# Two more chains for the first image's key offsets, and a later GELU in the first MLP unit

## The chip, the cores and the metric

The kernel runs on one core of a Trainium2 chip. The metric is the device time of the whole kernel in microseconds, in one launch; data is float32 throughout.

## The reference

An image batch x of shape (2, 512, 32, 32) goes through two layers. The first is a deformable attention block with an MLP, the second a plain self-attention. What the change touches lies in the first:

```python
q = _gconv1x1(_bn(x), qw)                                  # 8 groups of 64 channels
off = conv(q as 16 images of 64 channels, off_dw_w, stride 4, pad 1, depthwise)   # 6x6 taps, 8x8 out
off = gelu(off + off_dw_b); off = tanh(einsum('bchw,oc->bohw', off, off_pw_w)) * 4
kv = _grid_sample(xn, grid + off)                          # 64 sampled keys for each group
k, v = _gconv1x1(kv, kw), _gconv1x1(kv, vw)
pos = grid_q[:, :, None] - grid_kv[:, None]                # 1024 queries x 64 keys x 2
bias = sign(pos) * log1p(abs(pos))
bias = relu(relu(bias @ cpb_w1) @ cpb_w2) @ cpb_w3         # 2 -> 128 -> 128 -> 1
attn = softmax(q k^T / 8 + bias); x = x + out_w (attn v) + out_b
h1 = gelu(mlp_w1 _bn(x) + mlp_b1); x = x + mlp_w2 h1 + mlp_b2     # 512 -> 2048 -> 512
```

The second layer is softmax attention over the 1024 positions with four 512 x 512 projections and a residual sum.

## The kernel before, in words

Channels stand on the 128 partitions, so each image has four chunks (b, k) of 128 channels, two groups of 64 in each.

**The main loop.** The bias network takes most of the time. It runs over 256 slots s (one pass of the last loop in the attention part): 16 groups of 16 slots, four keys to a slot, and both images, so that a chunk is needed for 32 slots: chunk (0, 0) in slots 0 to 31, (0, 1) from 32, (0, 2) from 64, (0, 3) from 96, (1, 0) from 128 and so on. In a slot VectorE makes the first hidden layer h two slots ahead (`st_layer1`, L674, into three buffers); TensorE multiplies it by the 128 x 128 weights into four tiles ps of two PSUM banks (L691), of which three buffers exist; ScalarE evicts the four tiles (L701 and L703, into rx, ub and others); VectorE joins them in pairs (`st_sum`, L711); accumulating DMAs on the POOL queue and copies on the SP queue add them over partitions; 22 or 27 slots later TensorE contracts them to the scores (L821). Every fourth slot ScalarE makes tables ta and tb for the next (L654, L662).

**The background.** Beside this a Python generator `bg` does what the later groups need. In each slot whose number allows it, one step is taken, and what it issues is placed behind the second pair of evictions. It runs `chain(ci)` and then `sample(ci)` for each entry of the list CHAINS, in order. A chain has one chunk (K = 1) or two (K = 2). It normalises and projects q, forms the 36 tap products of the depthwise convolution on ScalarE, 12 at a time (`prod`, L381), sums them on VectorE (L396, L401), applies GELU on ScalarE (L405, with a table load), forms the offsets on TensorE (L420, L421) and tanh, log and positions. `TAPS[ci]` says how many taps go into one step; each `yield` ends a step. The result goes to DRAM (`fdr`), from where `load_tables` takes it in the slot with s % 4 = 0 ahead of its use: for chunk (0, 2) in slot 60, for (0, 3) in 92, for (1, 0) in 124. `sample` gathers the keys and makes k and v. The softmax steps of finished groups (`tails`) take every second slot until 60 and then those with s % 4 > 0. Every engine works its own instructions in the order of the program; ScalarE and VectorE serve the loop, the background and the softmax steps out of one queue each.

**The MLP.** Eight units (two images, four parts of the 2048 hidden channels) follow. `layer1` computes a unit's hidden part by a seven-product scheme; six of its products are split again by the same scheme in three sets (`twice`). `twice` orders all steps by a number: set g's products stand at 7 g + 0, 1, 3, 4, 6, 9, 12 (products 1, 2, 6, 5, 7, 4, 3), and other work is put in by its own number. Products 1, 6, 7 and 4 of a set accumulate in one PSUM bank, and each is copied out by ScalarE (L166, L170, L172, L176) before the next may add to it. The hidden blocks go through GELU on ScalarE (L1092). In unit 0, called with `early`, the seventh product is made ahead of all others and parked in r3; `merge` adds it to c11 and applies the GELU to block 0.

The functions that the change touches, and the places that call them:

Of the kernel before, what the change touches and what calls it, by code (L numbers as in the profile page):

```python
# [22 lines left out]
KS = 6  # L23
NG = 16

CHAINS = [[(0, 0)], [(0, 1)], [(0, 2), (0, 3)], [(1, 0), (1, 1)], [(1, 2), (1, 3)]]
TAPS = [36, 6, 4, 3, 3]
NU = 4
INV_BN = 1.0 / (1.0 + 1e-5) ** 0.5
FMAX = 3.4028234663852886e38  # L30
# [27 lines left out]
def conv_seq_kernel(ctx: ExitStack, tc: tile.TileContext, x, xt, kst, pst, cst, vec, wsm, outw, w1, w2, wl, wlt, brow, out):  # L58
# [30 lines left out]
    dp = ctx.enter_context(tc.tile_pool(name="dp", bufs=1, space=bass.MemoryType.DRAM))  # L89
    fdr = [dp.tile([2 * len(g), 4, 2 * W, KT], F32, name=f"fdr{i}") for i, g in enumerate(CHAINS)]  # L90
    chain_of = {c: (i, g.index(c)) for i, g in enumerate(CHAINS) for c in g}
    gdr = [dp.tile([P, NCH, C], F32, name=f"gdr{i}") for i in range(2)]
# [43 lines left out]
    def plus(out, a, b_, op=ALU.add):  # L136
        nc.vector.tensor_tensor(out, a, b_, op)  # L137
# [69 lines left out]
    with tc.tile_pool(name="lp", bufs=2) as lp:  # L207
# [111 lines left out]
        def chain(ci):  # L319
            G = CHAINS[ci]  # L320
            K = len(G)
            (b, k0), n = G[0], 128 * K
            for i in range(K):
                k = k0 + i
# [37 lines left out]
            if ci == 0:  # L362


                taps = sorted(range(KS * KS), key=lambda t: any(a in (0, KS - 1) for a in divmod(t, KS)))
                for m, t in enumerate(taps):
                    for src, dst in pieces(t, acc[:, m % 3]):
                        if m < 3:
                            nc.vector.tensor_scalar(dst, src, col("dww", t), None, ALU.mult)
                        else:  # L370
                            nc.vector.scalar_tensor_tensor(dst, src, col("dww", t), dst, ALU.mult, ALU.add)
            else:


                prod = ph.tile([P, 12, 2, 8, 8], F32, tag="xnt", name="prod")
                nc.gpsimd.memset(prod, 0.0)
                for m in range(3):
                    pr = prod[:, :, 0:K] if K == 2 else prod[:, :, m % 2 : m % 2 + 1]
                    for t in range(12):
                        for src, dst in pieces(12 * m + t, pr[:, t]):  # L380
                            nc.scalar.activation(dst, src, AF.Copy, scale=col("dww", 12 * m + t))  # L381
                        if t % TAPS[ci] == TAPS[ci] - 1:
                            yield
                    rows = ((0, 8, 0, 12),)
                    if m != 1:
                        rows = ((1, 8, 0, 12), (0, 1, 6, 12)) if m == 0 else ((0, 7, 0, 12), (7, 8, 0, 6))
                    for y0, y1, t0, t1 in rows:
                        for k in range(K) if y1 - y0 < 8 else (slice(0, K),):
                            src, dst = pr[:, t0:t1, k, y0:y1, :], acc[:, m, k, y0:y1, :]
                            if y1 - y0 < 8:  # L390
                                src, dst = (src.rearrange("p t y x -> p (y x) t"),
                                            dst.rearrange("p y x -> p (y x)"))
                            else:
                                src, dst = (src.rearrange("p t k y x -> p (k y x) t"),
                                            dst.rearrange("p k y x -> p (k y x)"))
                            nc.vector.tensor_reduce(dst, src, AX.X, ALU.add)  # L396
                    if m < 2 and K == 2:
                        yield
            af = acc.rearrange("p a k y x -> p a (k y x)")
            for i in (1, 2):  # L400
                nc.vector.tensor_tensor(af[:, 0], af[:, 0], af[:, i], ALU.add)  # L401
            if ci > 0:
                yield
            gof = ph.tile([P, K, J], F32, tag="gof", name="gof")
            nc.scalar.activation(  # L405
# [74 lines left out]
        def sample(ci):  # L480
            G = CHAINS[ci]
            K = len(G)
# [18 lines left out]
            for i, (b, k) in enumerate(G):  # L501
# [32 lines left out]
                nc.vector.tensor_tensor(kv, kv, uv, ALU.add)  # L534
                if i + 1 == K and ci + 1 < len(CHAINS):
                    xn0.append(load(*CHAINS[ci + 1][0]))
                yield
# [343 lines left out]
        bg = later()  # L881
# [4 lines left out]
        for s in range(NS):  # L886
            if s > 0:
                st_sum(s - 1, 2)
            for _, go, a in sorted(due.get(s, ()), key=lambda e: e[0]):
                go(a)  # L890
            if s % 4 == 0 and s // 4 + 1 < 4 * NG:
                load_tables(s // 4 + 1)
            if s + 2 < NS:
                st_layer1(s + 2)
            st_layer2(s)


            if s % 4 == 0 and s // 4 + 1 < 4 * NG:
                with tc.issue_after(evicted[s][0]):
                    st_tables(s // 4 + 1)  # L900
            st_sum(s, 0)

            if bg is not None and (s % 4 or s < 60):
                with tc.issue_after(evicted[s][1]):
                    next(bg, None)
            if bg is not None and state.get(len(CHAINS) - 1, 0) is None:

                bg = None
                php.__exit__(None, None, None)
                opp = tc.tile_pool(name="op", bufs=1, side="right")  # L910
                op = opp.__enter__()
                op0 = op_blocks(
                    0, op.tile([P, 3, 2, 512], F32, name="op0x"), op.tile([P, 3, 2, 256], F32, name="op0w")
                )
                ready = s
            if bg is None and s > ready and (s - ready) % 4 == 0 and (s - ready) // 4 <= 8:
                i = (s - ready) // 4 - 1
                if i < 4:
                    spread(op0[1], (i,))
                else:  # L920
                    fold(nc.vector, op0[0], which=(i - 4,))

            if tails and (s % (2 if s < 60 else 4) or s >= NS - NSL):
                with tc.issue_after(evicted[s][s % 4 == 0]):
                    if next(tails[0], 0) is not None:
                        tails.pop(0)
            for t in (27, 22):
                if s % NSL == t % NSL and s >= t and (s - t < FULL) == (t == 27):
                    st_layer3(s - t)
                    tails.append(softmax_steps((s - t) // NSL))  # L930
# [37 lines left out]
    with ExitStack() as top, tc.tile_pool(name="wp", bufs=1) as wp:  # L968
# [120 lines left out]
        def layer1(p, we, w, xb, xe, hm, others=(), early=False):  # L1089
            def gelu(blk, src, scale=1.0):  # L1090
                for m in range(2):
                    nc.scalar.activation(  # L1092
                        hm[:, blk, m, :], src[:, m, :], AF.Gelu,
                        bias=col("mb1", 4 * p + 2 * (blk // 2) + m), scale=scale,
                    )

            c11, c12, c21, c22, r5, r3 = (hm[:, j] for j in range(6))

            def weights(q, j):
                a = FIRST_W[PARTS[q][0]]  # L1100
                return [inner_w(w, we, a, a - 1)[j]]

            def moving(q, j):
                b_ = FIRST_X[PARTS[q][1]]
                return [inner_x(xb, xe, b_, b_ - 1)[j]]

            def dest(g, m, h):
                return hm[:, 2 * g : 2 * g + 2, m, 256 * h : 256 * h + 256]

            def done(g):  # L1110
                if g == 0:
                    plus(c12, c12, c11)
                elif g == 1:
                    plus(c22, c22, c12)
                    plus(c21, c21, c22)
                    gelu(2, c21, -1.0)
                else:
                    plus(c22, c22, r5)
                    gelu(3, c22, -1.0)
                    plus(c12, c12, r5)  # L1120
                    plus(c12, c12, r3)
                    gelu(1, c12)

            def second():
                ps = mq.tile([P, 2, 512], F32, tag="ps2", name="sw")
                product(w, xb)(ps, 0, 0)
                plus(c11, c11, ps)
                gelu(0, c11)

            def first():  # L1130
                ps = mq.tile([P, 2, 512], F32, tag="ps2", name="sw")
                product(w, xb)(ps, 0, 0)
                nc.scalar.copy(r3, ps)

            def merge():
                plus(c11, c11, r3)
                gelu(0, c11)

            plain = ((-1, first), (13.5, merge)) if early else ((21, second),)
            twice(mq, ((1, 6), (4, 7), (5, 3)), weights, moving, dest, done, (*plain, *others))  # L1140
            spread([hm[:, j] for j in range(7)])

# [52 lines left out]
        for i, (b, p) in enumerate(units):  # L1195

            j, k = divmod(i, NCH)
# [397 lines left out]
```

## Time and profile before

| what | value |
|---|---|
| median of 3 runs | 2628.18 us (2627.46 to 2630.05) |
| the profiled execution, its own time | 2629.82 us |
| its span, first to last instruction | 2628.1 us |
| TensorE matmul, busy | 2604.5 us, 99% of the span |
| VectorE busy | 2304.5 us, 88% |
| ScalarE busy | 1747.0 us, 66% |
| POOL busy | 980.0 us, 37% |
| mean granted TensorE clock | 0.997 |
| main loop, slots 0 to 255 | 38.3 to 1892 us after the start |

Busy times are unions over an engine's instructions. The record of TensorE has two entries for each matmul, so a slot has 64 of line L691. The span differs from the execution's time by what lies outside the first and last instruction, 1.7 us. Times in the text are counted from the first instruction. In a line of a timeline the first number is the start, the second the duration, and in brackets stand the idle time before it and what ended that.

### The profile page before, as it was taken

The page shows a single profiled execution, that of the slowest core. Times are in us where ns is not written, and L with a number is a line of the kernel's source. Part 1 is how long each engine was busy: PE and PEld are TensorE (multiplying, and loading weights), DVE is VectorE, ACT ScalarE, POOL GpSimd, SP SyncE. Part 2 cuts the span into 40 slices and gives each one's busy share as a digit, 9 for nine tenths or more (in the row PEclk, how much of TensorE's full clock was granted, in tenths as well). Part 3 has the DMA queues.
Part 4 walks back from the last instruction along what each step waited for, and adds up shares of the span by engine and source line. Part 5 has one row for each costly group of instructions (what it writes and reads, how often), then busy time and mean ns, then how long its engine had stood idle before and what let it go on. Part 6 is the DMA issues. An engine that isn't in the chain of part 4 may idle for free.

```text
span 2628.1 us, 48899 instructions
## 1 busy us (share of the span) xinstructions
PE 2604.5 (99%) x19648; PEld 1015.4 (39%) x19648; DVE 2304.5 (88%) x1446; ACT 1747.0 (66%) x2324; POOL 980.0 (37%) x1121
## 2 busy tenths in 40 slices
PE   9999999999999999999999999999999999999999
PEld 3332322233333333323333332332355665646556
DVE  6999999999999999999999999898776587666656
ACT  5887887888887888887887777777633242224041
POOL 1344444444444444444444454333322334200100
PEclk9999999999999999999999999999999999999999
DMA  5889988999999999899998999778777768400202
GB/s 187 174 190 196 202 183 183 193 197 194 187 196 193 194 200 196 180 190 200 193 197 182 193 194 193 166 167 179 159 194 161 153 138 174 93 16 0 72 0 56
DMA packets 177602, 428.27 MB, mean 163 GB/s; under 512 B 30016, under 2 KB 78288, under 8 KB 174688
## 3 DMA queue, kind: packets, MB, share of 16 engines
q0 software_dynamic: 107392, 273.09, 58.0%
q1 hardware_dynamic: 69552, 151.75, 17.4%
q8 instruction: 155, 2.54, 0.4%
q14 instruction: 71, 0.58, 0.1%
q10 hardware_dynamic: 432, 0.31, 0.0%
HBM read 82.16 MB, written 6.55 MB: 34 GB/s over the span
## 4 chain that ended last, share of the span: by engine, by line
PE 87%; DVE 5%; issue 4%; DMA 2%; POOL 2%; ACT 1%; DVEq 0%; POOLq 0%; ACTq 0%
PE ps L691 58%; PE sw L1073 7%; PE sw L160 7%; PE sw L1244 7%; PE sw L1020 2%; PE sw L1342 2%; DMA u<-uc 1%; PE psg L593 1%; DVE h L674 1%; POOL u L730 1%; PE sim L821 1%; DVE hm L137 1%; DVE ub L711 1%; PE psx L1320 1%; PE pkv L530 0%
## 5 line engine op out<-in xcount | busy, mean ns | idle before, releaser
L691 PE MATMUL ps<-h,cw 128*32 128x512 f32 x16384 | 1775.1, 593 | 8.2 <-ACT rx L701 6.3
L674 DVE CUSTOM_DVE_ANT_1 h<-ta,tb 128x4096 f32<-128x4096 f32 (+1 forms) x257 | 1131.4, 4403 | 28.9 <-PE ps L691 23.2
L691 PEld LDWEIGHTS ps<-h,cw 128*32 128x32 f32 x16384 | 532.3, 110 | 1219.1 <-issue 1140.4
L701 ACT ACTIVATE rx<-ps,sc 128x1024 f32<-128x1024 f32 x512 | 567.9, 1109 | 149.0 <-PE ps L691 111.1
L730 POOL DMA_DIRECT2D u<-u x397 | 408.5, 1505 | 16.8 <-DMA u<-ub 13.8
L703 ACT ACTIVATE ub<-ps,sc 128x1024 f32<-128x1024 f32 x256 | 308.2, 1204 | 91.7 <-PE ps L691 90.3
L711 DVE SCALAR_TENSOR_TENSOR ub<-rx,sc,ub 128x1024 f32<-128x1024 f32 x256 | 327.4, 1279 | 10.7 <-ACT ub L703 10.7
L713 POOL DMA_DIRECT2D uo<-ub x127 | 112.1, 883 | 576.9 <-DVE ub L711 529.8
L1073 PE MATMUL sw<-hm,w2t 128*128 128x512 f32 x448 | 194.4, 593 | 0.3 <-DVE hm L125 0.2
L703 ACT ACTIVATE uo<-ps,sc 128x1024 f32<-128x1024 f32 x128 | 154.1, 1204 | 46.8 <-PE ps L691 43.9
L711 DVE SCALAR_TENSOR_TENSOR uo<-rx,sc,uo 128x1024 f32<-128x1024 f32 x128 | 163.7, 1279 | 3.3 <-ACT uo L703 3.2
L730 POOL DMA_DIRECT2D u<-uc x126 | 125.9, 1254 | 22.8 <-DMA u<-uc 20.2
L713 POOL DMA_DIRECT2D uc<-ub x64 | 55.5, 867 | 200.3 <-DVE ub L711 176.9
L1073 PEld LDWEIGHTS sw<-hm,w2t 128*128 128x128 f32 x448 | 84.8, 190 | 104.4 <-issue 97.9
L713 POOL DMA_DIRECT2D u<-ub x64 | 56.3, 879 | 184.4 <-DVE ub L711 181.6
L137 DVE TENSOR_TENSOR hm<-hm,sw 128x512 f32<-128x512 f32 x79 | 57.3, 732 | 77.2 <-PE sw L160 51.8
L730 POOL DMA_DIRECT2D uc<-uc x63 | 112.0, 1778 | 2.0 <-DMA uc<-ub 2.0
L730 POOL DMA_DIRECT2D uc<-uo x63 | 101.9, 1618 | 9.3 <-DMA uc<-uo 8.2
L1408 POOL DMA_DIRECT2D xs<-rs x6 | 7.2, 1200 | 257.9 <-DVE rs L137 257.9
L730 POOL DMA_DIRECT2D u<-uo x63 | 90.7, 1440 | 19.3 <-DMA u<-uo 15.6
L703 ACT ACTIVATE u<-ps,sc 128x1024 f32<-128x1024 f32 x64 | 77.0, 1203 | 25.6 <-PE ps L691 21.3
L654 ACT ACTIVATE ta<-fb,vs 128x512 f32<-128x512 f32 (+1 forms) x65 | 89.3, 1377 | 5.9 <-DMA fb<-fdr 5.9
(297 smaller groups left out, 2626.6 us busy)
## 6 DMA issues: line engine op xcount, KB each, us to landing
uo<-ub POOLq DMA_DIRECT2D x127, 512.0 KB, 5.4
fb<-fdr SPq DMA_DIRECT2D x64, 512.0 KB, 5.7
u<-ub POOLq DMA_DIRECT2D x64, 512.0 KB, 6.3
uc<-ub POOLq DMA_DIRECT2D x64, 512.0 KB, 6.0
u<-u POOLq DMA_DIRECT2D x63, 256.0 KB, 6.9
u<-uo SPq DMA_DIRECT2D x63, 256.0 KB, 5.7
u<-uo POOLq DMA_DIRECT2D x63, 256.0 KB, 7.6
uc<-uc POOLq DMA_DIRECT2D x63, 256.0 KB, 8.5
```

The source lines that it names most:

```text
L137: nc.vector.tensor_tensor(out, a, b_, op)
L160: nc.tensor.matmul(bank[:, e, :], w, x, start=(q in (1, 2, 5) and e == k == 0), stop=True, skip_group_check=True,)
L654: nc.scalar.activation(ta.rearrange("p j x -> p x j")[:, :, j0:j1], fb[:, 0, :, j0:j1], AF.Identity, bias=col("cb1"), scale=col("w1x"),)
L674: nc.vector._custom_dve(TENSOR_ADD_SAT, out=h1[:, y : y + step].rearrange("p y t x -> p (y t x)"), in0=a.unsqueeze(1).to_broadcast([P, ste ...
L691: nc.tensor.matmul(ps[32 * q : 32 * q + 32, h, :], cw2[:, 32 * z : 32 * z + 32], h1[:, 16 * h : 16 * h + 16, q, :], start=True, stop=True,)
L701: nc.scalar.activation(o, ps, AF.Relu, bias=sc[:, 4 + z : 5 + z])
L703: nc.scalar.activation(o, ps, AF.Relu, bias=sc[:, 4 + z : 5 + z], scale=sc[:, z : z + 1])
L711: nc.vector.scalar_tensor_tensor(r[1], r[0], sc[:, z : z + 1], r[1], ALU.mult, ALU.add)
L713: nc.gpsimd.dma_start(out=sums[s][1], in_=sums[s][3], accum_op=ALU.add)
L730: nc.gpsimd.dma_start(out=out, in_=in_, accum_op=ALU.add)
L1073: nc.tensor.matmul(ps[:, m, :], w[:, a, k, m * P : (m + 1) * P], x[:, b_, k, :], start=(k == 0), stop=(k == 1),)
L1244: nc.tensor.matmul(ps[:, m, :], w[:, a, k, c + m * P : c + (m + 1) * P], x[b_][:, k, :], start=(k == 0), stop=(k == nk - 1),)
```

## The change

The second and the third entry of the list of chains were one chunk and two chunks of the first image; now each of the four chunks of the first image has a chain of its own. Chunks (0, 2) and (0, 3) are thus processed one after the other with sampling between them, each with one-chunk instructions and six taps to a step. In a chain of two chunks, all of which belong to the second image now, a step ends between the sums of the first and of the second chunk of each full set of rows of the first and last tap group. From the third chain on a step that issues nothing follows the last sum, ahead of the GELU. The background takes a step in every slot until 124 instead of 60, and leaves out the slots with s % 4 = 0 only from there on. In unit 0 of the MLP the sum of the parked product stays at 13.5, and the GELU of its block moves from 13.5 to 19.5.

```diff
-CHAINS = [[(0, 0)], [(0, 1)], [(0, 2), (0, 3)], [(1, 0), (1, 1)], [(1, 2), (1, 3)]]
-TAPS = [36, 6, 4, 3, 3]
+CHAINS = [[(0, 0)], [(0, 1)], [(0, 2)], [(0, 3)], [(1, 0), (1, 1)], [(1, 2), (1, 3)]]
+TAPS = [36, 6, 6, 6, 3, 3]
...
                             nc.vector.tensor_reduce(dst, src, AX.X, ALU.add)
+                            if K == 2 and k == 0 and t1 - t0 == 12:
+                                yield
                     if m < 2 and K == 2:
                         yield
...
             for i in (1, 2):
                 nc.vector.tensor_tensor(af[:, 0], af[:, 0], af[:, i], ALU.add)
             if ci > 0:
+                yield
+            if ci > 1:
                 yield
             gof = ph.tile([P, K, J], F32, tag="gof", name="gof")
...
-            if bg is not None and (s % 4 or s < 60):
+            if bg is not None and (s % 4 or s < 124):
                 with tc.issue_after(evicted[s][1]):
                     next(bg, None)
...
-            def merge():
-                plus(c11, c11, r3)
-                gelu(0, c11)
-
-            plain = ((-1, first), (13.5, merge)) if early else ((21, second),)
+            plain = ((21, second),)
+            if early:
+                plain = (-1, first), (13.5, lambda: plus(c11, c11, r3)), (19.5, lambda: gelu(0, c11))
```

## The prediction

> **What bounds the kernel now.** I read the page's busy shares first, then who TensorE waited for, then the granted clock around its two longest waits, then the timelines of ScalarE (ACT) and VectorE (DVE) there.
>
> ```profile
> PE 2604.5 (99%) x19648; PEld 1015.4 (39%) x19648; DVE 2304.5 (88%) x1446; ACT 1747.0 (66%) x2324; POOL 980.0 (37%) x1121
> ```
>
> ```profile
> PE ps L691 <- ACT rx L701: 6.3, 7, 2.4
> ...
> PE sw L160 <- ACT hm L166: 3.8, 1, 3.8
> ```
>
> TensorE idles 23.6 us of 2628.1, so only two things can move the time: matmul work added or removed, and what is left of its waits. One wait of 2.4 us and one of 3.8 us are most of them. The view by windows, cut at these two, has the granted clock behind ACT and POOL (the third column from the right):
>
> ```profile
> 414.08:421.84 7.76, 5.33 (x52) 1.43 (x44) 7.76 (x6) 4.30 (x6) 2.54 (x4) 1.00 1.04 217
> 421.84:430.02 8.18, 8.18 (x40) 3.43 (x44) 8.18 (x4) 4.82 (x5) 5.42 (x9) 0.58 0.99 221
> ...
> 1965.44:1969.24 3.80, 0.00 (x0) 0.00 (x0) 0.35 (x2) 3.68 (x5) 0.85 (x1) 1.00 0.40 69
> 1969.24:1972.88 3.64, 3.64 (x9) 2.92 (x10) 0.67 (x1) 0.59 (x1) 0.00 (x0) 0.53 0.00 0
> ```
>
> After each wait the clock is halved. 0.58 over 8.18 us is 2 x 0.42 x 8.18 = 6.9 us at half speed, so 3.4 us lost; 0.53 over 3.64 us is 3.4 us at half speed, so 1.7 us lost. The waits cost 2.4 + 3.4 = 5.8 us and 3.8 + 1.7 = 5.5 us: 11.3 us in all.
>
> The first wait lies in slot 52 of the 256-slot loop (a slot is one pass over s):
>
> ```profile
> 411.17 1.11 ACT L701 ACTIVATE rx<-ps,sc 128x1024 f32<-128x1024 f32 x1 [2.70 <-DVE ub L711]
> ...
> 419.42 0.40 ACT L405 ACTIVATE gof<-acc,vs 128x128 f32<-128x128 f32 x1 [2.59 <-DVE acc L401]
> 420.68 1.11 ACT L701 ACTIVATE rx<-ps,sc 128x1024 f32<-128x1024 f32 x1 [0.85 <-DVE ub L711]
> ```
>
> ```profile
> 412.20 2.65 DVE L396 TENSOR_REDUCE acc<-prod 128x56 f32<-128x672 f32 x2
> 414.78 4.41 DVE L674 CUSTOM_DVE_ANT_1 h<-ta,tb 128x4096 f32<-128x4096 f32 x1
> ```
>
> The GELU stands ahead of an eviction and waits for a sum (L401) queued behind a 4.41 us h; but the eviction after it also waits for DVE. So DVE is late, and the GELU only sits on top. DVE needs 4.41 + 2 x 1.28 less three overlaps of 0.07 = 6.73 us a slot, TensorE 6.87 (64 records): DVE regains 0.14 us a slot, and more where TensorE has other work. By the timeline, the h of slot 44 was done 9.6 us before TensorE's first matmul of that slot, that of slot 52 only 4.2 us. Between them lie the tap sums of the two-chunk chain 2, 8.97 us of L396. At 4.2 us of lead TensorE stalls; the last 2.6 us of reduces less 0.14 put it 2.5 below that, and the wait was 2.4.
>
> The second wait is in the first MLP unit:
>
> ```profile
> 1965.48 0.60 ACT L176 ACTIVATE hm<-sw 128x512 f32<-128x512 f32 x1 [1.99 <-PE sw L160]
> 1966.09 1.28 ACT L1092 ACT_TABLE_LOAD   x1
> 1967.39 1.33 ACT L1092 ACTIVATE hm<-hm,vs 128x512 f32<-128x512 f32 x2
> 1968.63 0.56 ACT L166 COPY hm<-sw 128x512 f32<-128x512 f32 x1
> 1969.24 3.63 PE L160 MATMUL sw<-xe,w1e 128*128 128x256 f32 x8 [3.80 <-ACT hm L166]
> ```
>
> Product 6 adds into the bank of product 1, so it waits for the copy L166, which stands behind a table load and two GELUs.
>
> **What the Trainium skill says.** "TensorE: Matmul & The Clock Gate", part 1 (the HAM clock gate): after an idle window of about 3.4 us the clock falls to half until a busy window has passed, the windows running freely. The trace agrees in size (half speed for 3.4 and 6.9 us), but a wait of 2.4 us sufficed once and one of 1.9 us (at 1815) did not. "ScalarE: Activation LUTs", "What ACT_TABLE_LOAD costs": 1283 ns a load; the trace has 1.28 us. It adds a drain of 1.38 us, which the trace doesn't show: the GELU starts 0.02 us after the load. "VectorE: DVE Perf Modes", the TRN2 errata: a fixed cost per instruction, so halves cost more than the whole. Here a reduce of half the size takes 1.546 us against 2.965.
>
> **The change part by part.**
>
> *Chunks (0,2) and (0,3) as chains of their own.* In the loop they now do what chain 1, a one-chunk chain, does in slots 11 to 35 of before. Its L396 time was 4.67 us, and the lead fell to 6.4 us, with no TensorE wait. By the generator's steps the sums move from slots 42, 46, 50 to 39, 41, 43 for (0,2) and 65, 67, 69 for (0,3). The first starts at a lead of about 10 us and ends at about 6.4. So the wait at 421.84 goes, and with it the half clock: -5.8 us. I take it that the unprofiled runs of before have this half clock too; where they do not, only 2.4 is gained.
>
> TensorE pays for the split: the offset products (L420, L421) take 1.68 us for one chunk (189.66 to 191.34) and 1.99 us for two (810.07 to 812.06): 2 x 1.68 - 1.99 = +1.4 us, on the path. The projections and samplings are per chunk in both. ACT gets three more table loads of 1.28 us and more, shorter tap products, POOL one more memset of 2.2 us and SP two small stores; all lie under TensorE's 6.87 us slots (ACT's evictions leave 2.6 us of each free; POOL is busy 37%). Without that cover the loads alone cost 3.8 us and the memset 2.2 us.
>
> *Tap products.* In slot 40 eight and then six products plus the tables made TensorE wait 0.5 us (341.89). Now six a slot: -0.3 us (0 to -0.5).
>
> *Empty steps at the sums, and for two chunks a step between theirs.* The GELU comes a slot after its last sum. For the second image's first chain the sums lie in slots 95/96, 101, 106/107 (before 89, 95, 102); the same 9.2 us in 11 slots instead of 13. From a lead of 9.06 at slot 97 I get 9.06 + 12 x 0.14 + 0.7 + 1.1 + 0.9 (TensorE's own transposes and scores) - 8.9 = about 4.4 by slot 110: 0.2 above the stall. I take 0, up to +0.7. For the last chain, 145/146, 153, 159/161 instead of 143, 150, 157: four waits of 1.1 us together (1147 to 1210) lose most: -0.7 (0 to -1.1).
>
> *Chain steps in every slot up to 124.* Slots 64, 68, 88, 92, 104 get tables (1.9 us net) and six or so chain instructions (1.8) in one slot: 3.6 to 3.8 us. Slots 12, 16, 36, 48 of before carried 3.6 to 3.9 so without a wait. Slot 114 gets an Ln between two Exp, three loads and 4.3 us in one place; a half slot leaves 1.3 us, the banks some 2.2 more: 0.8 us late. Together +1.1 (0 to +2.5). The background ends at slot 193 instead of 187; what follows has over 5 us of lead there.
>
> *GELU of unit 0 at 19.5.* By the program's order ACT then runs L176, L166, load, GELU, L170, GELU. L166 then ends at 1966.07 - 0.09 (overlap) + 0.56 = 1966.54, and TensorE goes on at 1966.59: 1.15 us idle instead of 3.80, -2.65. Too short for half clock: -1.7. The load and first GELU (1.28 + 0.72) end near 1968.5, L170 at 1969.0, before product 7 needs it at 1969.3. What is late next is L170, by a margin of 0.3 us. Sum -4.4 (-2.0 to -5.5).
>
> Sum: -5.8 + 1.4 - 0.3 - 0.7 + 1.1 - 4.4 = -8.7 us. The profiled execution took 2629.8, 1.6 above the median of 2628.2; from the median, 2619.5.
>
> **Rivals.** 0.2% is 5.3 us, about what a measurement of this kernel tells from no change.
>
> *The DVE deficit moves.* The denser sums of slots 95 to 107 push the lead through 4.2 us, and a wait of 2.4 with its 3.4 of half clock returns near slot 110. For: a margin of 0.2 us. Against: the same work made none in slots 89 to 105. -8.7 + 5.8 = -2.9: 2625.3.
>
> *Unit 0 only moves its wait.* If L170 or the GELU that product 2 reads is late by a microsecond or two, or a window still halves the clock, 3 us of the 4.4 return: 2622.5. For: 0.3 us of margin. Against: DVE's chain to that GELU is unmoved.
>
> *The change does little of what it says:* the scheduler could have put the GELU back ahead of L166. The order of the program's instructions excludes it, so it gets no chance of its own.
>
> *Slower: ACT overflows in slots with tables.* ACT holds the banks when tables, chain and softmax steps of neighbouring slots exceed the 2.2 us that three banks cover. One overflow of 2.4 us draws 3.4 of half clock. It decides from three such places among slots 64, 68, 88, 92, 104, 114: 3 x 5.8 = 17.4 against the gain of 9.8 without ACT's 1.1: 2628.2 - 9.8 + 17.4 = 2635.8. For: slot 67 already carries 2.8 us. Against: the loads of 3.6 to 3.9 that made no wait before.
>
> **Numbers.** Chances: the forecast 0.68, DVE 0.13, unit 0 0.13, ACT 0.06. Low end: all of both waits and small ones, no new ones, -5.8 + 1.4 - 0.5 - 1.1 - 5.5 = -11.5 and some 2 us for half-clock phases: 2614.5. High end past the DVE rival: 2626.0. Faster takes most of the forecast and half of unit 0's rival: 0.73; same 0.21; slower 0.06.
>
> **What would show it.** Right: no TensorE wait over 1 us and no half clock before slot 220; a wait of about 1.2 us for L166 in unit 0 at clock 1.00; TensorE's busy sum lower by about 4 us (5.1 of half clock less 1.4). Wrong: waits of rx for ub near slot 110, of ps for rx in slots 64 to 114, or a granted clock at half after any of them.

## The result and the profile after

| kernel | median, us | range, us | runs |
|---|---|---|---|
| before, beside the changed kernel | 2628.18 | 2625.24 to 2631.47 | 9 |
| changed | 2619.60 | 2617.88 to 2624.03 | 9 |

The ratio, taken over all runs, is 0.9972, 95% interval 0.9961 to 0.9982: 7.4 us less, 4.7 to 10.2. The medians themselves differ by 8.6. The nine times of the changed kernel lie in two groups, five from 2617.88 to 2619.60 and four from 2622.82 to 2624.03, so that the median is the highest of the lower group. The profiled execution of the changed kernel took 2619.14 us, its span is 2617.3 us, 10.8 us shorter than that of before. Line numbers after the chains are higher by 2 to 4 (L691 is now L695).

The page's first part and then the answer on what TensorE waited for:

```profile
PE 2599.8 (99%) x19660; PEld 1011.9 (39%) x19660; DVE 2301.5 (88%) x1459; ACT 1752.4 (67%) x2362; POOL 980.2 (37%) x1122
```

```profile
PE ps L695 <- ACT rx L705: 3.3, 3, 1.9
...
PE sw L160 <- ACT hm L166: 1.2, 1, 1.2
```

Evictions of rx were waited for 6.3 us in seven waits before; now 3.3 us in three, of which 0.41 and 1.89 lie at the end of the loop, where before had the same two. The copy L166 is waited for 1.2 us instead of 3.8. The windows that answer to the two places, with the granted clock in the third column from the right:

```profile
414.77:428.50 13.73, 13.73 (x132) 4.16 (x128) 13.70 (x9) 11.67 (x14) 8.29 (x10) 1.00 0.99 204
...
1960.28:1963.90 3.62, 3.62 (x16) 2.95 (x16) 1.36 (x3) 3.06 (x4) 0.85 (x1) 1.00 0.42 72
```

The first is slots 52 and 53: TensorE works through all 13.73 us, where before it was idle for 2.4 and at half clock for 6.8. The second begins where product 6 of unit 0 starts again, now at full clock. ScalarE in unit 0, by the timeline:

```profile
1959.15 0.60 ACT L176 ACTIVATE hm<-sw 128x512 f32<-128x512 f32 x1 [1.99 <-PE sw L160]
1959.64 0.58 ACT L166 COPY hm<-sw 128x512 f32<-128x512 f32 x1
1960.24 1.28 ACT L1096 ACT_TABLE_LOAD   x1
1961.54 0.72 ACT L1096 ACTIVATE hm<-hm,vs 128x512 f32<-128x512 f32 x1
1962.16 0.57 ACT L170 COPY hm<-sw 128x512 f32<-128x512 f32 x1
```

L166 ends at 1960.22 and the load stands behind it; product 6 starts at 1960.28, 1.16 us after TensorE fell idle. L170 ends at 1962.73, 0.24 us ahead of product 7 (1962.97).

Of the 10.8 us between the two profiles, 5.6 had been gained when TensorE began the last slot (1884.73 against 1879.15), 4.3 came in unit 0 (from its first product to the first of unit 1: 51.80 against 47.48), and 0.7 from a shorter wait for the last scores (1.44 against 0.70).

### The profile page after: what moved, and what is told of

Its sections match the earlier page's. It is cut to its first block, busy times and chain, and to the rows that moved or that the text cites. A ratio compares the mean times of both kernels' runs of the same rounds, so it can differ in the third digit from the quotient of the medians.

```text
span 2617.3 us, 48989 instructions
## 1 busy us (share of the span) xinstructions
PE 2599.8 (99%) x19660; PEld 1011.9 (39%) x19660; DVE 2301.5 (88%) x1459; ACT 1752.4 (67%) x2362; POOL 980.2 (37%) x1122
## 4 chain that ended last, share of the span: by engine, by line
PE 92%; DVE 4%; issue 2%; ACT 1%; DMA 1%; POOL 0%; DVEq 0%; ACTq 0%; POOLq 0%
PE ps L695 64%; PE sw L1077 7%; PE sw L1246 7%; PE sw L160 6%; PE sw L1024 2%; PE sw L1344 2%; PE psg L597 1%; DVE hm L137 1%; PE sim L825 1%; PE psx L1322 1%; DVE h L678 0%; DMA uc<-uc 0%; ACT rx L705 0%; PE sim L806 0%; PE pt L842 0%
## 5 line engine op out<-in xcount | busy, mean ns | idle before, releaser
L695 PE MATMUL ps<-h,cw 128*32 128x512 f32 x16384 | 1773.3, 592 | 5.2 <-ACT rx L705 3.3
L695 PEld LDWEIGHTS ps<-h,cw 128*32 128x32 f32 x16384 | 529.7, 110 | 1216.8 <-issue 1144.1
L734 POOL DMA_DIRECT2D uc<-uc x63 | 106.3, 1687 | 2.3 <-DMA uc<-ub 2.3
L734 POOL DMA_DIRECT2D uc<-uo x63 | 102.8, 1632 | 10.8 <-DMA uc<-uo 10.4
L707 ACT ACTIVATE uc<-ps,sc 128x1024 f32<-128x1024 f32 x64 | 77.0, 1203 | 21.6 <-PE ps L695 18.4
```

What stands on the lines that cost most here:

```text
L695: nc.tensor.matmul(ps[32 * q : 32 * q + 32, h, :], cw2[:, 32 * z : 32 * z + 32], h1[:, 16 * h : 16 * h + 16, q, :], start=True, stop=True,)
L707: nc.scalar.activation(o, ps, AF.Relu, bias=sc[:, 4 + z : 5 + z], scale=sc[:, z : z + 1])
L734: nc.gpsimd.dma_start(out=out, in_=in_, accum_op=ALU.add)
```

## The experiments

**The chains alone, and the GELU alone.** Two kernels, each with one half of the change:

```diff
 # first: changed kernel, but in unit 0 as before
-                plain = (-1, first), (13.5, lambda: plus(c11, c11, r3)), (19.5, lambda: gelu(0, c11))
+            plain = ((-1, first), (13.5, merge)) if early else ((21, second),)
 # second: kernel before, with the new lines of unit 0
-            plain = ((-1, first), (13.5, merge)) if early else ((21, second),)
+                plain = (-1, first), (13.5, lambda: plus(c11, c11, r3)), (19.5, lambda: gelu(0, c11))
```

> The chains, steps and slots of the change alone; in unit 0 the GELU stays at 13.5 as before. Theory (two independent gains, one in the loop from VectorE's lead and one in unit 0): TensorE's 2.4 us wait in slot 52 and the half clock after it are gone, the 3.8 us wait for L166 and the half clock after it are still there; about 5.6 us less than before (the start of unit 0's idle time came 6.3 us earlier in the profile of the changed kernel, 0.75 of it at the last scores). Rival (the loop's gain is given back, all comes from unit 0): 0 to -1 us.

> The GELU of unit 0 at 19.5 alone; chains as before. Theory: the loop has its 2.4 us wait and half clock as before; in unit 0 a wait of 1.15 us at full clock; about 4.3 us less than before. Rival (what was saved in unit 0 returns in layer 2, whose GELUs wait for VectorE anyway): the wait of unit 0 falls but less than 2 us are left at the end of unit 0.

The GELU alone: ratio 0.9982 (0.9975 to 0.9989), 4.7 us less (2.9 to 6.6). Its unit 0, up to the first product of unit 1, takes 47.48 us as in the changed kernel, so nothing is given back in layer 2. This half came as expected.

The chains alone: ratio 0.9995 (0.9987 to 1.0003), between 3.4 us less and 0.8 more; 5.6 were expected. By its time this half alone can't be told from no change, and its 1.3 us lie nearer to the rival's 0 to 1 than to 5.6. The wait of slot 52 is gone in its profile, as expected. But the last scores of the loop came late:

```profile
PE sim L825 <- issue: 5.0, 1, 5.0
PE sw L160 <- ACT hm L166: 3.8, 1, 3.8
```

```profile
1886.68:1891.64 4.96, 0.01 (x2) 0.04 (x2) 1.28 (x1) 2.72 (x8) 1.71 (x2) 1.00 0.50 107
1891.64:1895.30 3.66, 3.66 (x11) 1.13 (x14) 0.00 (x0) 0.00 (x0) 0.00 (x0) 0.53 0.63 119
```

TensorE is idle for 5.0 us and then at half clock for 3.4. The loop is the changed kernel's, instruction by instruction; there this wait was 0.7 us. On POOL's queue the last accumulation into u, which waits for the landing of those before it, was issued at 1888.99, against 1884.28 in the changed kernel (this kernel first):

```profile
1888.99 0.82 POOL L734 DMA_DIRECT2D u<-uc  x1 [4.90 <-DMA u<-uc]
```

```profile
1884.28 0.82 POOL L734 DMA_DIRECT2D u<-uc  x1 [5.00 <-DMA u<-uc]
```

So the same loop ended 4 to 6 us later in this execution (4.3 us more of waiting, and 1.7 lost at half clock). The accumulations before it landed later too; what delayed them was not traced. The 13 times of this kernel have a gap between 2624.6 and 2627.4; this profile is of an execution of 2627.47, and none of the lower group was profiled. The late scores are one part of what is missing. Another is in the 5.6 us themselves: 3.4 of them are the half clock after slot 52 in the first profile of before, which other profiles show shorter or not at all (below).

**An empty step ahead of the GELU, without the split.**

```diff
             if ci > 0:
                 yield
+            if ci == 2:
+                yield
             gof = ph.tile([P, K, J], F32, tag="gof", name="gof")
```

> The kernel before with one empty step ahead of the GELU of chain 2 (two chunks), and nothing else; steps behind it shift by a slot. Theory (VectorE is late with h and sums by 2.5 us, the GELU only sits on top): a TensorE wait of 2 to 2.5 us stays at slot 52 or 53, ended by an eviction rx that waited for the sum ub, though the GELU has moved on; the time is that of before within 1.5 us. Rival (the GELU waiting at the head of ScalarE's queue makes the wait): the wait and the half clock go, 5 to 6 us less.

Ratio 1.0007 (0.9998 to 1.0015). ScalarE's timeline:

```profile
414.45 1.21 ACT L705 ACTIVATE ub<-ps,sc 128x1024 f32<-128x1024 f32 x1
420.80 1.11 ACT L703 ACTIVATE rx<-ps,sc 128x1024 f32<-128x1024 f32 x1 [5.14 <-DVE ub L713]
```

No GELU and no table load stand between the two evictions, and rx still waits for VectorE's sum ub, now 5.14 us in one piece. TensorE's wait at 421.97 is 2.43 us, as before (2.44):

```profile
421.97 3.64 PE L693 MATMUL ps<-h,cw 128*32 128x512 f32 x32 [2.43 <-ACT rx L703]
```

This settles that VectorE is late there, and that the GELU only sat on top. A second wait, of 4.79 us at 490.22, is this kernel's own: chain 2 stores its result in slot 58 instead of 57, and the tables of slot 60 read it from there:

```profile
487.41 1.27 ACT L656 ACTIVATE ta<-fb,vs 128x512 f32<-128x512 f32 x1 [5.85 <-DMA fb<-fdr]
```

This second wait would hide a gain of 5 us, so the time of this kernel decides nothing here; the profile does.

**Twice the sums in one of the new chains.**

```diff
-                            nc.vector.tensor_reduce(dst, src, AX.X, ALU.add)
+                            for _ in range(2 if ci == 2 else 1):
+                                nc.vector.tensor_reduce(dst, src, AX.X, ALU.add)
```

> The changed kernel with every tap sum of chain 2 (chunk (0,2)) issued twice, 4.7 us more on VectorE in slots 39 to 43 and nothing else changed. Theory (the lead of VectorE decides): the lead, 6.2 us at slot 46 in the changed kernel, falls to the 4.2 us at which TensorE stalls, and a TensorE wait of 2 to 3 us in all comes back near slots 45 to 47, ended by an eviction that waits for VectorE, though an empty step stands ahead of the GELU. Rival (the split into smaller steps and the empty step are what removed the wait): no TensorE wait over 0.5 us there.

The tap sums of this stretch take 9.04 us instead of 4.72. The lead of h, counted as in the prediction, falls to 1.0 us at slot 46, below the 4.2 that were expected, and TensorE waits 1.65 us at 377.91 and 0.31 at 354.59: 2.0 us in all, the lower end of what was expected. The waits in this stretch, and ScalarE's timeline, which names the cause:

```profile
PE ps L696 <- ACT rx L706: 2.0, 2, 1.7
```

```profile
374.73 0.35 ACT L410 ACTIVATE gof<-acc,vs 128x64 f32<-128x64 f32 x1
376.74 1.11 ACT L706 ACTIVATE rx<-ps,sc 128x1024 f32<-128x1024 f32 x1 [1.66 <-DVE ub L716]
```

The GELU found its sum ready and ran at once; the eviction behind it waits for VectorE. The split, the small steps and the empty step are all there, and the wait is back. What the change moved in slots 36 to 60 is VectorE's load.

**Without the empty steps.**

```diff
-                            if K == 2 and k == 0 and t1 - t0 == 12:
-                                yield
...
-            if ci > 1:
-                yield
             gof = ph.tile([P, K, J], F32, tag="gof", name="gof")
```

> The changed kernel without the empty steps ahead of the GELU and without the step between the two chunks' sums; four own chains, steps in every slot and unit 0 as changed. Theory (the spread over chains does the work, the empty steps little): no wait over 1 us in slots 36 to 110; the waits of the last chain (slots 151 to 155) return with about 1 us in all; the Ln of the second image's first chain comes in slot 109, ahead of the softmax's Exp at 114, so the wait of 0.96 us at slot 114 is gone. Time within 1.5 us of the changed kernel. Rival (the empty steps carry the gain): a wait of 2 us or more at a GELU.

Ratio 0.9973 (0.9962 to 0.9984), not to be told from the changed kernel's. The wait at slot 114 is gone (ScalarE's work of that slot; TensorE is by then in slot 115). In the second image's chains two came instead: 0.79 us at 803.10 (TensorE in slot 105) and 1.71 at 1151.75 (slot 153), more than the 1 us expected. At both, rx waits for ub:

```profile
800.68 0.40 ACT L405 ACTIVATE gof<-acc,vs 128x128 f32<-128x128 f32 x1 [0.50 <-DVE acc L401]
801.94 1.11 ACT L701 ACTIVATE rx<-ps,sc 128x1024 f32<-128x1024 f32 x1 [0.85 <-DVE ub L711]
...
1150.59 1.11 ACT L701 ACTIVATE rx<-ps,sc 128x1024 f32<-128x1024 f32 x1 [3.51 <-DVE ub L711]
```

So the one-chunk chains of the first image do without empty steps, and the two-chunk chains of the second are spared waits of 2.5 us by them and by the step between their sums. The two were taken out together, so which of them does it stays open. The kernel loses less than that, since the wait at slot 114 is gone.

**One slot earlier.**

```diff
-            if ci > 1:
+            if ci > 2:
                 yield
```

> The changed kernel without the empty step in chain 2 alone, so that all later steps come a slot earlier and the Ln of the second image's first chain falls in slot 113, one ahead of the softmax's first Exp. Theory (three table loads in one place, Exp to Ln to Exp, make the 0.96 us wait of slot 114): two loads fewer in that slot, the wait is gone, 1 us less than the changed kernel. Rival (VectorE's lead, 4.6 us at slot 110, makes it): the wait stays near slot 110 to 114.

In the changed kernel the Ln (L463) falls between two Exp of the softmax (L859) in slot 114, three table loads within 7 us:

```profile
869.07 1.28 ACT L859 ACT_TABLE_LOAD   x1
...
872.92 1.28 ACT L463 ACT_TABLE_LOAD   x1
874.21 0.31 ACT L463 ACTIVATE fe<-fe 128x128 f32<-128x128 f32 x1
874.52 1.28 ACT L859 ACT_TABLE_LOAD   x1
```

With the shift, two loads are left, one before the Exp, and the wait of 0.96 us at 877.32 is gone, as it is in the run before, where the Ln also comes elsewhere: the loads made it. But 0.67 us came at 566.07 (TensorE in slot 73) and 0.59 at 1233.47, so the waits add up to no less. The ratio is 0.9965 (0.9952 to 0.9978), not to be told from the changed kernel's.

**Another place for the parked product.**

```diff
-                nc.scalar.copy(r3, ps)
+                nc.scalar.copy(hm[:, 6], ps)
...
-                plain = (-1, first), (13.5, lambda: plus(c11, c11, r3)), (19.5, lambda: gelu(0, c11))
+                plain = (-1, first), (13.5, lambda: plus(c11, c11, hm[:, 6])), (19.5, lambda: gelu(0, c11))
```

> The changed kernel with unit 0's parked product in block 6 of hm instead of block 5 (r3), so that product 1 of the third set, which is copied over block 5 by L166, need not come after VectorE's sum that reads the parked product. Theory (the 1.16 us left in unit 0 is L166 queued behind L176 because of this one buffer): L166 stands before L176, that wait is gone, 1.2 us less than the changed kernel. Rival (the bank or the table load sets it): a wait of about 1 us stays at product 6 or appears at product 7.

L166 of the third set now stands ahead of L176, and the wait is gone:

```profile
1957.30 0.59 ACT L166 COPY hm<-sw 128x512 f32<-128x512 f32 x1 [0.27 <-PE sw L160]
1959.03 0.60 ACT L176 ACTIVATE hm<-sw 128x512 f32<-128x512 f32 x1 [1.14 <-PE sw L160]
```

Unit 0 takes 46.86 us, 0.6 less than in the changed kernel, not the 1.2 of the wait. Shorter waits stand in its place, of 0.12 us for VectorE inside products 6 and 5 and of 0.21 for L170 at product 7, so the rival came true in part:

```profile
1962.18 1.13 PE L160 MATMUL sw<-xb,w1x 128*128 128x256 f32 x4 [0.21 <-ACT hm L170]
```

The median is 2617.62 us (2617.25 to 2618.01, 5 runs), the ratio 0.9965 (0.9953 to 0.9978). It is the fastest of all by its median, though its interval overlaps that of the changed kernel.

**Both of these.** The diffs of the last two together.

> The shift of the run before with unit 0's product parked in block 6. Theory: both waits are gone, some 2.1 us less than the changed kernel, 2616 to 2618 us where the last scores come in time. Rival: as in the two single runs, one of the waits only moves.

2619.60 us, ratio 0.9968 (0.9956 to 0.9981); 2616 to 2618 were expected. The waits at slot 114 and at L166 are gone, those of 0.67 and 0.60 us of the shift are there, and the wait for the last scores was 1.4 us. No run gives a reason for the shift.

**The same kernels once more.** No edit.

> The kernel before once more, for a second profile of it. Theory[...]: the 2.4 us wait of slot 52 and the 3.8 us wait of unit 0 are there to 0.05 us; half clock follows the second, and the first only by chance. Rival (the half clock belongs to both waits in every execution, as in the first profile): 6.8 us of half clock after slot 52 again.

> The kernel before, a third profile. Theory and rival as for the second: the two waits the same to 0.05 us, the half clock after slot 52 by chance.

> The changed kernel once more. Theory (its two groups of times, 2618 to 2620 and 2623 to 2624, differ by a late wait for the last scores, 0.7 us in its first profile and 5.0 us in that of the run with the chains alone): where the time is over 2622, this wait is over 3 us and half clock may follow; where it is under 2620.5, it is under 2 us. Rival: the groups differ by waits elsewhere in the loop.

> The changed kernel, a third profile. Theory and rival as for the second: all of what differs between its executions lies in the wait for the last scores and in half clock after it.

The wait of slot 52 was 2.42 and 2.44 us, that of unit 0 3.80 and 3.80. What followed slot 52 differs. In the first profile the clock was 0.58 in the window 421.84 to 430.02; the same window in the two later ones, b_look1 first:

```profile
421.84:430.02 8.18, 7.78 (x68) 3.06 (x72) 8.18 (x5) 6.59 (x8) 5.42 (x9) 1.00 0.99 224
```

```profile
421.84:430.02 8.18, 8.18 (x56) 3.08 (x52) 8.18 (x4) 5.51 (x6) 5.42 (x9) 0.79 1.00 228
```

That is 6.8, 0 and 3.4 us at half speed. With the two experiments that kept this wait (the GELU alone and the empty step: none in either), five profiles have 6.8, 3.4, 0, 0, 0: 1.0 us lost on average, not 3.4. After the wait of unit 0, half clock of 3.4 us came in all five profiles that have it. The two executions of the changed kernel took 2618.11 and 2616.74 us, with waits for the last scores of 0.61 and 0.46 us. They fit the theory, but neither fell into the group over 2622 us, so a late last score is seen in one execution of the chains alone, and what makes the upper group of the changed kernel stays open.

## Why the prediction was right

The number was 2619.5, the measurement 2619.6. By its own steps:

- **Unit 0, -4.4 us.** Measured -4.32 (51.80 to 47.48), and -4.7 (2.9 to 6.6) as a kernel of its own. The residual wait was put at 1.15 and is 1.16; that L170 would be next, with 0.3 us to spare, is 0.24. This term is right in mechanism and size.
- **Slot 52, -5.8 us.** The mechanism, VectorE's lead running out under the two-chunk sums, is shown by the empty step (wait unchanged) and by the doubled sums (wait back). The lead of 6.4 us expected at its lowest in the new chain was 6.2 at slot 46; in the chain of chunk (0, 3) it fell to 4.9 at slot 72, without a wait. The size is wrong for an ordinary execution: the term "with it the half clock: -5.8 us" took the half clock of one profile for a property of the kernel. Five profiles give 2.4 + 1.0 = 3.4 us. The text named the other case, -2.4, and did not choose it.
- **Small waits, -0.3 - 0.7 + 1.1 = +0.1 us.** Measured between the two first profiles: -0.49 (slot 41) - 1.11 (1147 to 1210) + 1.07 (695.85 and 877.32) = -0.5. The wait at slot 114 was put at 0.8 and is 0.96. The five slots with tables and chain steps made 0.12 us between them.
- **TensorE's extra offset products, +1.4 us.** The two new groups take slots of 8.66 us (46 and 72), 1.8 over the bare 6.87, as chain 1 did. In b_look1 slot 52, at full clock, takes 11.60 us with its wait of 2.42, so the two-chunk chain cost 2.3, and the difference is 1.3. The term stands.
- **The sum.** The over-sized half clock, 2.4 us, is partly met by 0.6 us of small waits. By the ratio the change is -7.4 (-10.2 to -4.7), an interval that holds -8.7. The profiles' difference of 10.8 contains the half clock of before. That the number falls within 0.1 us is luck: the changed kernel's own nine times spread over 6 us, and had one more of them fallen in the upper group, their median would be above 2622. What the times show apart from noise is the gain of unit 0; that of the chains is shown by the waits in the profiles, and as a time of its own it is not.

Three readings in the prediction are off without moving its result. The two waits are 6.2 of the 23.6 us in which TensorE idles, not most of them; another 6.2 lie behind its last matmul. The sum for VectorE's slot comes to 6.76 us as written; the 6.73 is what the timeline has (405.47 to 412.20). And the lead by slot 110 comes to 4.5 us as written, not 4.4.

Of the rivals, the deficit of VectorE did not reach TensorE in slots 95 to 110: the lead at slot 110 was 4.6 us. Without the empty steps and the step between the sums it did, by 0.8 and 1.7 us. But 4.2 us is no fixed point of stalling, as the prediction took it to be: in the changed kernel the lead was 4.2 at slots 155 and 163 and TensorE did not wait there; without the empty steps it waited at a lead of 5.9 in slot 105 and of 5.0 in slot 153. ScalarE did not overflow by the 2.4 us of its rival; its largest overflow is the 0.96 us at slot 114. Unit 0 did not move its wait. What the prediction did not see is the wait for the last scores, which was 0.5 to 5.0 us in the profiles of the same loop and can hide part of what the loop gains.

## What to carry to other kernels

When one engine runs ahead of another by a fixed number of buffers, count that lead in microseconds slot by slot: what drains it and what refills it tells where a wait is near, and whether the instruction on which the wait is seen is its cause. Don't take the lead at one wait for a threshold; here waits of 0.8 us and more behind VectorE came at leads of 1.0 to 5.9 us. A waiting instruction at the head of a queue may only sit on top of a late engine; moving it is a cheap test. Take the price of a half clock after a wait from several profiles, since executions of one program differ in it.

## What the runs showed of the hardware

The half clock after a TensorE wait, over the fourteen profiles: waits of 1.65 to 1.89 us, none; 2.42 to 2.44 us, in two of five profiles, for 3.4 or 6.8 us; 3.80 us, in five of five, always 3.4 us; 4.79 and 4.95 us, 3.4 us each. Unexpected was that 2.4 us are enough at all, and that they were once followed by 6.8 us of half clock where 5.0 us were followed by 3.4. In all nine cases the clock fell 2.9 to 5.1 us after TensorE went idle, in eight of them when it was already working again. At the end of each profile, where TensorE has nothing left to do for 6 us, it fell 2.3 to 5.1 us after the last matmul.

Also unexpected: in the same loop, the chain of accumulating DMAs that ends it ran 4.7 us later in one execution than in another (1888.99 against 1884.28 for its last accumulation into u), with no instruction of the loop changed.
